# Query parts stored once and repeated on loading, the value ring in the place of projection weights, and the first maximum pass planned into phase one

## The chip, the cores and the metric

The kernel runs on one core of a Trainium2 chip. Its engines are named as in the profile: PE (TensorE, matrix products; PEld is its loading of weights), DVE (VectorE), ACT (ScalarE), POOL (GpSimd) and SP (SyncE), which here issues every DMA. The metric is device time in microseconds of one execution. Beside it the profile gives the granted clock of TensorE, as a share of full speed.

## The reference

The reference is one decoder block over 32 sequences `b` of 128 positions by 512 features, with three layer normalisations, each after a residual sum:

```python
x = _layernorm(x + _L0_attn_ref(x, Wq, Wk, Wv, Wo))
x = _layernorm(x + _L0_xattn_ref(x, ctx_2048, ctx_2048, gamma))
x = _layernorm(x + _L0_ffn_ref(x, w1, b1, ln_g, ln_b, w2, b2))
```

- `_L0_attn_ref` is causal self-attention with 16 heads of 32 features and rotary positions.
- `_L0_xattn_ref(q, k, v, gamma)` works across features: the 128 positions are cut into 8 heads of 16, and in each head `einsum('bhdq,bhdl->bhql')` contracts those 16 positions, so the scores of a head are 512 by 512. Softmax over the last axis, then `einsum('bhql,bhdl->bhdq')`; keys and values are both the context.
- `_L0_ffn_ref` is a feed-forward layer of 512 to 2048 to 512 with weights rounded to -1, 0, 1 and activations rounded to 8 bits; SiLU, exact GELU and a layer normalisation lie between its two products.

## The kernel before

The work is in two phases, each written out as operations with a kind, a planned cost, a priority and their buffers (`pl.op("PE.mx", cost, fn, ins, outs, prio)`). A list scheduler (class `Plan`) orders them: of all kinds' next operations it takes the one with the earliest planned start, in steps of `slack`, and between equals the one of lowest priority; to the priority it adds an offset for the kind from the tables `OFF1` (phase one) and `OFF2` (phase two). It emits the instruction at once, and then fixes the order on every engine. So on the chip each engine runs a fixed list in order, and SP's list of DMAs is one of them. Every DMA issue waits, besides its own data, for the landing of the DMA eight issues earlier on SP.

**Phase one** (0 to about 563 us) takes the sequences in turn: the projections (L346, PE, `banka`), self-attention (L447 to L500), the output projection with weights wo (L346 again), the residual `ya` (L505), statistics and `x1` (L519, POOL). `x1` is stored as it is in `x1_d` (L521), and by `split3` cut into three bfloat16 parts whose sum is x1: a high part (L354, ACT), a difference (L357, POOL), a second part (L359, ACT), and the rest (L361, POOL), all in one tile `sp`. The parts are stored by L364. The context is split likewise into `k_d` and reshaped into `c_d`. The feed-forward weights are quantised on the side.

A product of two split numbers needs six pairs of parts. The kernel makes them one matrix product with a contraction over 96 rows (6 pairs by 16 positions): it stores the query parts in the order 0, 1, 2, 0, 1, 0 and the context parts in the order 0, 0, 0, 1, 1, 2, so that row block `s` of the one meets row block `s` of the other. So each sequence has six stores of 128 KB to `q_d` and six to `k_d`, and half a sequence (four heads) is loaded by one DMA of 96 rows of 4 KB, 384 KB, into a tile `qp` or `kp` (L656; rings of `NQ` = 4 tiles). Rows 96 and 97 are extra: `kp` has ones there, loaded from `ones_d` (L587), and `qp` gets the negated maxima.

**Phase two** (from about 563 us) works in 64 units, sequence `b` by half `g`. A unit has two passes:

- `b1_`, the maximum pass: 16 products of 96 rows (L677, tile `mx`), 16 maximum reductions on DVE (L681, into `mt`), a transpose on PE (L691), and its negation split into `mhi` and `mlo` (L694, L695), which two DMAs of 4 KB put in rows 96 and 97 of `qp` (L700).
- `b2_`: 16 products of 98 rows (L756, `sT`), which give scores less their maximum; 16 exponentials on ACT (L759, `ex`); products with the value tile `cT` (L766, `acc`), whose second half is set to one by a memset (L616) so that the same product gives the sum of the exponentials; a copy (L773) and a store to `F` (L777).

After the two units of a sequence come the division and layer normalisation (L838 to L848, over `F`, `den`, `rd`, `rden`, `num`), the feed-forward layer (up L925, down L1009, with transposing DMAs `q1T` and `q2T`) and the store of the output.

The seam: when the last projection operation has been planned, a function `early()` runs. It closes the pool of the projection weights wqk and wv, opens the pool `qk` in their place, and issues there the ones and the loads of the first four units:

```python
for i in range(NQ):
    nc.sync.dma_start(k[NPR:NROW], ones_d)
    for t, d in ((k, k_d), (q, q_d))[:2 if i < min(CFG['early'], NQ) else 0]:
        nc.sync.dma_start(t[0:NPR], d[i // 2]...)
```

The other tiles of phase two lie in pools (`smb`, `pb`, `cb`, `psb`) that are opened once phase one has been planned, and so in memory that phase one used. Among them are the three value tiles `cT` (the ring `vring`) with their memsets, in the pool `cb`. A tile there waits for the last instructions and DMAs of phase one that used the memory.

Of the kernel before, what the change touches and what calls it, by code (L numbers as in the profile page):

```python
# [11 lines left out]
F32 = mybir.dt.float32  # L12
# [30 lines left out]
Q_PARTS = (0, 1, 2, 0, 1, 0)  # L43
K_PARTS = (0, 0, 0, 1, 1, 2)
# [19 lines left out]

CFG = dict(y0e='Pool', x2be='Pool', q2T=1, q1=2, tb2=3, boost=1.0, bank_mT='mx', bank_q1T='m', bank_z='m', bank_q2T='mx', bank_py='m', early=5, ssv=1, NQ=4, cT=3, f=2, num=1, x1=2, rden=2, x2=2, nb=32, mx=3, sT=3, acc=1, m=1, ex=8, mTe='DVE', acce='ACT', q1e='ACT', q2e='ACT', lne='Pool', ye='Pool', sce='Pool', mxw=1, stw=1, pair=1, z=3, xb=3, slack=0.05, last_lne='DVE', last_ye='DVE', last_sce='DVE', last_y0e='DVE', last_bank_mT='sT', last_bank_q1T='m', last_bank_z='sT', last_bank_q2T='mx', last_bank_py='sT', zm='PPPP', last_zm='FFFP', q1m='p', q2m='ad', last_q1m='d', last_q2m='ad')
OFF2 = {'SP.const': -264.67, 'x.kq': 390.3, 'SP.v': 77.29, 'PE.mx': -381.13, 'DVE.mx': 126.92, 'PE.mT': -632.22, 'DVE.mT': 8.23, 'SP.m': -156.28, 'PE.sT': -531.43, 'ACT.ex': -687.83, 'PE.pv': 37.38, 'ACT.acc': -737.17, 'SP.f': 49.63, 'SP.fd': 1119.71, 'SP.fn': 725.19, 'SP.fx': 343.0, 'DVE.rd': -172.57, 'SP.fr': -316.31, 'SP.fb': 17.98, 'Pool.y': -355.28, 'DVE.y': -82.99, 'Pool.yn': -277.59, 'DVE.c1': -57.25, 'Pool.c1': -358.01, 'Pool.c1m': -627.03, 'Pool.q1a': -78.8, 'Pool.x2b': 72.59, 'SP.q1T': -375.73, 'PE.c1': 39.79, 'DVE.z': -137.9, 'ACT.gelu': -406.78, 'DVE.nmu': -80.22, 'ACT.sq': -333.32, 'Pool.zn': -48.07, 'Pool.zt': 303.63, 'Pool.zb': -221.61, 'ACT.sq2': 252.58, 'DVE.am2': 91.79, 'Pool.c2': -682.87, 'Pool.c2m': -291.19, 'ACT.q2a': -262.61, 'DVE.q2a': -514.12, 'SP.q2T': 382.04, 'PE.c2': 86.97, 'DVE.c3': 17.23, 'Pool.c3': -278.83, 'Pool.c3n': 302.38, 'SP.out': 77.71, 'SP.kq': -42.69, 'DVE.yn': -735.62, 'DVE.c1m': 785.24, 'DVE.q1a': 467.22, 'DVE.zn': 550.15, 'DVE.zb': -508.13, 'DVE.c2m': -306.12, 'DVE.c3n': 99.96}
OFF1 = {'SP.x': 76.47, 'SP.w': -83.56, 'ACT.w': 1251.46, 'DVE.wl': 97.39, 'DVE.w': 1455.82, 'SP.wq': 258.11, 'ACT.wq': -501.07, 'DVE.wq': -718.11, 'PE.wq': 497.75, 'ACT.xh': -83.03, 'Pool.xl': -493.52, 'PE.qkv': 642.06, 'DVE.rope': -749.29, 'Pool.rope': 726.68, 'ACT.v': -277.88, 'SP.cx': 161.38, 'ACT.cs': 561.27, 'Pool.cs': 151.36, 'Pool.cs3': 444.12, 'SP.cs': -169.59, 'SP.ct': -341.75, 'ACT.ct': 5.76, 'SP.cv': 657.35, 'PE.qkT': -233.53, 'DVE.qkT': -713.26, 'PE.sc': 223.31, 'DVE.mask': -673.03, 'ACT.exp': 343.93, 'DVE.rd': 481.16, 'DVE.pr': 893.48, 'PE.prT': -342.18, 'DVE.prT': 602.51, 'ACT.prT': 121.56, 'Pool.pr': 38.32, 'PE.pv': 403.29, 'ACT.oh': 297.53, 'DVE.ol': -241.16, 'PE.wo': 645.28, 'DVE.y': -873.41, 'Pool.y': 255.11, 'Pool.x1': -113.85, 'SP.x1': 730.76, 'ACT.xs': 299.8, 'Pool.xs': -1039.81, 'Pool.xs3': 582.54, 'SP.xs': 975.4}
C1 = dict(pace=15.0, xs=4, pr=5, prT=7, ra=3, qkT=4, sp=3, spr=2, xhe='ACT', lne='Pool', s1e='Pool', s2e='ACT', cxl=-0.5, wq=3.0, nb=32, wst=4, mm=3, tr=3, sc=4, scc=1.1, po=1, pc=4, spe='ACT', cte='ACT', s3e='Pool', qke='DVE', pre=['DVE', 'DVE', 'Pool', 'Pool'], prTe=['DVE', 'ACT', 'ACT', 'ACT'], wl=24.0, slack=0.02)
# [14 lines left out]
class Plan:  # L83
# [34 lines left out]
    def op(self, kind, cost, fn, ins=(), outs=(), prio=0.0, lat=None, rel=0.0, join=False):  # L118
# [5 lines left out]
        o.deps, o.new = [], []  # L124
# [96 lines left out]
def decoder_kernel(ctx: ExitStack, tc: tile.TileContext, x, xT, cx, cxT, wqkT, wvT, woT, gamma,  # L221
# [28 lines left out]
    q_d = [dram.tile([6, XD, XH, D], BF16, tag=f"qd{b}", name=f"qd{b}") for b in range(NB)]  # L250
    c_d = [dram.tile([P, XD, NC * XH], F32, tag=f"cd{b}", name=f"cd{b}") for b in range(NB)]
    k_d = [dram.tile([6, XD, XH, D], BF16, tag=f"kd{b}", name=f"kd{b}") for b in range(NB)]


    with ExitStack() as st1:
# [38 lines left out]
        for name in ("mm", "tr", "sc", "po"):  # L294
            pl.tag(name, C1[name], group="bank")
        pl.tag("part", 2, wts, (P, 16))

        def dma(kind, fn, kb, ins=(), outs=(), prio=0.0, rel=0.0):
            pl.op("SP." + kind, max(0.55, kb / 340), fn, ins, outs, prio, 2.2 + kb / 340, rel)
# [38 lines left out]
        def project(kind, pq, parts, w, sl, wb, prio):  # L338

            steps = [(a, t, c) for a, t in ((0, 0), (1, 0), (0, 1)) for c in range(NC)]  # L340
            m = C1['pc']
            for i in range(0, 12, m):
                def mm(i=i):
                    for k in range(i, i + m):
                        a, t, c = steps[k]
                        nc.tensor.matmul(pq.t, parts[a].t[:, c, :], w[t][:, c, sl], start=k == 0, stop=k == 11)  # L346
                used = [parts[0]] + ([parts[1]] if i + m > 4 else [])
                pl.op("PE." + kind, 0.236 * m, mm, used + [wb], (pq,), prio)

        def split3(kind, v, dst, parts, prio):  # L350
# [12 lines left out]
            for s, k in enumerate(parts):  # L363
                dma(kind, lambda s=s, k=k: nc.sync.dma_start(dst[s].rearrange("t h c -> h t c"), sp.t[:, k, :]), 131,  # L364
                    (sp,), (), prio)

        def context(b):
# [3 lines left out]
            split3("cs", t, k_d[b], K_PARTS, at)  # L371
# [114 lines left out]
        def stage_o(b):  # L486
# [35 lines left out]
            split3("xs", x1, q_d[b], Q_PARTS, at)  # L522
# [46 lines left out]
        for b in range(NB1):  # L569
            stage_q(b)  # L570
            context(b)
            stage_s(b)
            stage_o(b)
        pl.slack = C1['slack']
        NQ = CFG['NQ']
        kring, qring = [], []

        def early():

            st2.close()  # L580
            qk = pool(ctx, "qk", side="right")
            for i in range(NQ):
# [5 lines left out]
                for t, d in ((k, k_d), (q, q_d))[:2 if i < min(CFG['early'], NQ) else 0]:  # L588
                    nc.sync.dma_start(t[0:NPR], d[i // 2][:, :, 4 * (i % 2):4 * (i % 2) + 4, :].rearrange(
                        "s t h c -> (s t) h c"))  # L590
# [3 lines left out]
    sm2 = pool(ctx, "smb")  # L594
# [10 lines left out]
    NB2 = CFG['nb']  # L605
    NQ = CFG['NQ']
# [6 lines left out]

    vring = [cb.tile([P, 2 * XD, NC * XH], F32, tag=f"cT{i}", name=f"cT{i}") for i in range(CFG["cT"])]
    for t in vring:
        nc.gpsimd.memset(t[:, XD:], 1.0)  # L616
    pl.tag("cT", CFG["cT"], ring=vring)
    pl.tag("kp", NQ, ring=kring)
    pl.tag("qp", NQ, ring=qring)
    pl.tag("zq", 64, ring=[None] * 64)  # L620
    for name, shape, dtype in (
            ("mt", (P, 16), F32), ("mhi", (16, P), BF16), ("mlo", (16, P), BF16),
# [21 lines left out]
    Q, K, V, X2 = {}, {}, {}, {}  # L644

    def load(b):
        at = b
        for g in range(2):
            K[b, g], Q[b, g] = k, q = pl.buf("kp"), pl.buf("qp")
            h = slice(4 * g, 4 * g + 4)  # L650

            first = 2 * b + g < min(CFG['early'], NQ)

            def fetch(t, d, h=h, first=first):
                if not first:
                    nc.sync.dma_start(t.t[0:NPR], d[b][:, :, h, :].rearrange("s t h c -> (s t) h c"))  # L656
# [3 lines left out]
            dma("kq", lambda k=k, fetch=fetch: fetch(k, k_d), 393, outs=(k,), prio=at, rel=30.0 * b - 40.0)  # L660
            dma("kq", lambda q=q, fetch=fetch: fetch(q, q_d), 393, outs=(q,), prio=at, rel=30.0 * b - 40.0)
        V[b] = v = pl.buf("cT")
        dma("v", lambda: nc.sync.dma_start(v.t[:, 0:XD], c_d[b]), 262, outs=(v,), prio=at + 0.5, rel=30.0 * b)

    def b1_(b, g):

        at = b + 0.5 * g
        k, q = K[b, g], Q[b, g]
        mt, W = pl.buf("mt"), CFG['mxw']

        def unit(h, qc):
            sc = pl.buf("mx")
            p = at + 0.5 * (4 * h + qc) / 16

            def scores():
                for j in range(W):
                    nc.tensor.matmul(sc.t[:, j, :], q.t[0:NPR, h, (qc + j) * P:(qc + j + 1) * P], k.t[0:NPR, h, :],  # L677
                                     start=True, stop=True)
            pl.op("PE.mx", 0.222 * W, scores, (q, k), (sc,), p)
            i = 4 * h + qc  # L680
            pl.op("DVE.mx", 0.064 + 0.534 * W, lambda: nc.vector.tensor_reduce(mt.t[:, i:i + W], sc.t, AX.X, ALU.max),  # L681
                  (sc,), (mt,), p, join=True)
        for h in range(4):
            for qc in range(0, NC, W):
                unit(h, qc)
        shift(b, g, mt, at + 0.5)

    def shift(b, g, mt, at):

        hi, lo, pt, q = pl.buf("mhi"), pl.buf("mlo"), bank(b, 'mT'), Q[b, g]  # L690
        pl.op("PE.mT", 0.2, lambda: nc.tensor.transpose(flat(pt)[0:16, 0:P], mt.t, ident), (mt,), (pt,), at)  # L691

        def parts():
# [8 lines left out]

    def last(b):
        return b >= NB2 - CFG['tb2']

    def slow(b):

        return 2.0 if b >= NB2 - 2 else 1.0

# [375 lines left out]
```

## Time and profile before

| | |
|---|---|
| three runs | 1674.02, 1676.19, 1684.5 us; median 1676.19 |
| the profiled execution | 1675.28 us, its span 1673.5 us, granted clock 0.973 |
| PE busy | 1551.4 us, 93% of the span |
| ACT, DVE, POOL busy | 1432.7 (86%), 1383.9 (83%), 1251.5 us (75%) |
| DMA | 258.71 MB, 155 GB/s in the mean; 192 stores `qd<-sp` and 192 `kd<-sp` of 128 KB, 64 loads `qp<-qd` and 64 `kp<-kd` of 384 KB |

The page gives one execution. The span runs from the first to the last instruction; the execution's own time is 1.8 us longer. A row of a window table names a stretch of the span, then for each engine the microseconds it was busy in it and how many instructions it ran, the granted clock, the mean busy share of the 16 DMA engines and their rate. A line of waits names who waited, for whom, the sum in us, how often, and the longest. A line of a timeline gives start and length in us, the engine (SPq is SP issuing a DMA), the line in the kernel, the operation, its output and inputs, and how many such instructions in a row. Where one engine's in-order list holds an instruction that waits, all behind it wait too.

### The profile page before, as it was taken

How to read it: one execution, taken by the hardware profiler on the slowest of the kernel's cores; microseconds unless marked ns; L12 is line 12 of the kernel's file. 1: busy time of each engine (PE TensorE's matmuls, PEld its weight loads, DVE VectorE, ACT ScalarE, POOL GpSimd, SP SyncE). 2: the span in 40 equal slices, each digit the busy share in tenths (PEclk: the TensorE clock that was granted, in tenths of full speed). 3: DMA queues.
4: the chain of work that ended last, by engine and by line, in shares of the span. 5: the costliest groups of instructions: out<-in, count | busy, mean ns of one | idle time of the engine just before them, and what ended most of it. 6: DMA issues, size and time to landing. Idle time of an engine off the chain costs nothing.

```text
span 1673.5 us, 30270 instructions
## 1 busy us (share of the span) xinstructions
PE 1551.4 (93%) x9540; PEld 785.0 (47%) x9540; DVE 1383.9 (83%) x3315; ACT 1432.7 (86%) x2950; POOL 1251.5 (75%) x1679
## 2 busy tenths in 40 slices
PE   6999999999999799999999999999999999999844
PEld 4878777777778333333333333333333333333211
DVE  6877776777777678899999989899899999998674
ACT  4889989899976367999989989899999999998963
POOL 3777778777787404679879888878978888986772
PEclk8999999999999799999999999999999999999977
DMA  6476677766664654355455345545544544544221
GB/s 226 163 236 232 226 231 244 255 233 214 209 208 153 185 177 122 93 129 145 113 133 147 105 129 139 131 115 139 142 110 128 153 110 134 149 122 123 69 62 50
DMA packets 235680, 258.71 MB, mean 155 GB/s; under 512 B 110072, under 2 KB 159224, under 8 KB 235136
## 3 DMA queue, kind: packets, MB, share of 16 engines
q1 hardware_dynamic: 235520, 256.78, 52.8%
q8 instruction: 75, 1.23, 0.3%
q14 instruction: 85, 0.70, 0.1%
HBM read 142.41 MB, written 92.81 MB: 141 GB/s over the span
## 4 chain that ended last, share of the span: by engine, by line
PE 41%; DVE 18%; POOL 16%; DMA 9%; ACT 8%; issue 7%; SPq 1%; POOLq 0%; ACTq 0%; DVEq 0%
PE banka L346 12%; DVE mt L681 8%; PE acc L766 7%; PE sT L756 6%; POOL z L972 6%; PE mx L677 5%; PE m L925 2%; DVE am L998 2%; PE banka L477 2%; DMA qd<-sp 2%; POOL z L794 2%; PE banka L447 2%; ACT pr L465 1%; ACT ex L759 1%; PE banka L496 1%
## 5 line engine op out<-in xcount | busy, mean ns | idle before, releaser
L681 DVE TENSOR_REDUCE mt<-mx 128x1 f32<-128x512 f32 x1024 | 643.4, 679 | 54.9 <-PE mx L677 52.9
L759 ACT ACTIVATE ex<-sT 128x512 f32<-128x512 f32 x1024 | 533.9, 615 | 77.9 <-PE sT L756 74.4
L677 PE MATMUL mx<-kp,qp 96*128 96x512 bf16 x1024 | 336.9, 386 | 21.5 <-DVE mt L681 17.7
L756 PE MATMUL sT<-qp,kp 98*128 98x512 bf16 x1024 | 320.7, 385 | 15.9 <-DMA qp<-mlo 13.3
L766 PE MATMUL acc<-ex,cT 128*32 128x512 f32 x2048 | 289.4, 637 | 0.0
L465 ACT ACTIVATE pr<-pr,nm 128x128 f32<-128x128 f32 x512 | 198.9, 394 | 4.1 <-DVE nm L459 4.1
L756 PEld LDWEIGHTS <-kp 98*128 98x128 bf16 x1024 | 90.3, 98 | 223.7 <-issue 125.1
L677 PEld LDWEIGHTS <-qp 96*128 96x128 bf16 x1024 | 96.3, 98 | 195.5 <-issue 95.1
L972 POOL TENSOR_TENSOR z<-z,bb_b 128x512 f32<-128x512 f32 x119 | 154.4, 1301 | 0.3
L972 POOL TENSOR_TENSOR z<-z,g_b 128x512 f32<-128x512 f32 x119 | 153.5, 1297 | 0.5
L459 DVE CUSTOM_DVE_ANT_0 pr<-banka,cmask 128x128 f32<-128x128 f32 x512 | 111.0, 286 | 35.9 <-PE banka L447 35.2
L1009 PE MATMUL m<-w2q,q2T 128*128 128x512 fp8e4 x464 | 116.7, 385 | 16.4 <-DMA q2T<-q 16.4
L766 PEld LDWEIGHTS acc<-ex,cT 128*32 128x32 f32 x2048 | 70.6, 184 | 114.1 <-issue 108.8
L925 PE MATMUL m<-w1q,q1T 128*128 128x512 fp8e4 x464 | 119.1, 378 | 2.7 <-DVE z L928 1.3
L1009 PEld LDWEIGHTS <-q2T 128*128 128x128 f16 x512 | 51.0, 101 | 104.5 <-DMA q2T<-q 34.9
L465 ACT ACTIVATION_READ_ACCUMULATOR pr<-pr,nm 128x1 f32 x512 | 98.0, 191 | 0.0
L794 POOL TENSOR_SCALAR z<-z,nmu,rs 128x512 f32<-128x512 f32 x119 | 94.5, 801 | 1.8
L361 POOL TENSOR_TENSOR sp<-spr,sp 128x512 bf16<-128x512 f32 x64 | 76.7, 1200 | 20.3 <-ACT sp L359 18.2
L928 DVE SCALAR_TENSOR_TENSOR z<-m,dq,b_b 128x512 f32<-128x512 f32 x116 | 85.0, 733 | 1.8 <-PE m L925 1.5
L925 PEld LDWEIGHTS <-q1T 128*128 128x128 f16 x512 | 49.2, 97 | 76.1 <-issue 19.9
L846 POOL TENSOR_TENSOR num<-num,rden 128x512 f32<-128x512 f32 x29 | 37.1, 1278 | 62.3 <-DMA rden<-rd 62.2
L346 PE MATMUL banka<-wqkh,xh 128*128 128x512 f32 x256 | 73.9, 411 | 10.3 <-ACT xh L388 10.3
(152 smaller groups left out, 3247.9 us busy)
## 6 DMA issues: line engine op xcount, KB each, us to landing
kd<-sp SPq DMA_DIRECT2D x192, 128.0 KB
qd<-sp SPq DMA_DIRECT2D x192, 128.0 KB
kp<-kd SPq DMA_DIRECT2D x64, 384.0 KB
qp<-qd SPq DMA_DIRECT2D x64, 384.0 KB
F<-f SPq DMA_DIRECT2D x64, 256.0 KB
xt<-in_xT SPq DMA_DIRECT2D x32, 256.0 KB
xs<-in_x SPq DMA_DIRECT2D x32, 256.0 KB
ct<-in_cxT SPq DMA_DIRECT2D x32, 256.0 KB
```

What stands on the lines that cost most here:

```text
L346: nc.tensor.matmul(pq.t, parts[a].t[:, c, :], w[t][:, c, sl], start=k == 0, stop=k == 11)
L459: nc.vector.tensor_tensor_reduce(pr.t[:, c, :], sc.t[:, c * P:(c + 1) * P], cmask, -1.0, 3e38, ALU.add, ALU.min, nm.t[:, c:c + 1])
L465: nc.scalar.activation(pr.t[:, c, :], pr.t[:, c, :], AF.Exp, scale=-1.0, bias=nm.t[:, c:c + 1], accum_out=den.t[:, c:c + 1])
L677: nc.tensor.matmul(sc.t[:, j, :], q.t[0:NPR, h, (qc + j) * P:(qc + j + 1) * P], k.t[0:NPR, h, :], start=True, stop=True)
L681: pl.op("DVE.mx", 0.064 + 0.534 * W, lambda: nc.vector.tensor_reduce(mt.t[:, i:i + W], sc.t, AX.X, ALU.max), (sc,), (mt,), p, join=True)
L756: nc.tensor.matmul(sc.t[:, i, :], k.t[:, h, lc * P:(lc + 1) * P], q.t[:, h, :], start=True, stop=True)
L759: pl.op("ACT.ex", 0.052 + 0.426 * SW, lambda: nc.scalar.activation(ex.t[:, j:j + SW, :], sc.t, AF.Exp, scale=1.0 / XD ** 0.5), (sc,), (ex, ...
L766: nc.tensor.matmul(acc.t[32 * h:32 * h + 32, :], v.t[:, :, XH * lc + 4 * g + h], exs[h // 2].t[:, h % 2, :], start=lc == 0, stop=lc == NC - 1)
L794: pl.op(e + "." + p, cost + 0.1, lambda: en(e).tensor_scalar(o.t[:, sl], v.t[:, sl], sh.t, sc.t, ALU.add, ALU.mult), ins, outs, prio)
L925: nc.tensor.matmul(flat(pz)[:, i * 512:(i + 1) * 512], q1T.t[:, c, :], w1q[:, c, (n + i) * 512:(n + i + 1) * 512], start=c == 0, stop=c == ...
L972: pl.op(e + kind, 0.148 + 0.0021 * w if e == "Pool" else 0.05 + 0.00105 * w, lambda: en(e).tensor_tensor(t(), t(), other[:, sl], op), src, ...
L1009: nc.tensor.matmul(flat(py)[:, 0:D], q2T.t[:, c, :], w2q[:, c, :], start=c == 0, stop=c == NI - 1)
```

## The change

Three things are changed, and with them the planned order.

1. `q_d` holds each of the three query parts once, so a sequence has three stores to it and not six. A unit's query tile is filled by three DMAs: part 0 three times (48 rows), part 1 twice (32 rows), part 2 once (16 rows). The repetition is made by the DMA's source pattern (`to_broadcast`). The row blocks of `qp` now hold parts 0, 0, 0, 1, 1, 2, and the context parts are stored in the order that fits; there are still six context stores, grouped by part.
2. The value tiles `cT` with their memsets are made in `early()`, in the memory of wqk and wv, ahead of the ones.
3. The loads of the first four units are operations of phase one's plan and no longer issued inside `early()`, and the maximum pass of the first unit (`CARRY` = 1) is planned in phase one too, with phase one's PSUM banks. The pool `smb` with `mt`, `mhi`, `mlo` is opened at the start for that.

The offsets of all kinds in `OFF1` and `OFF2` have new values, the planned costs of the projection, of the stores and of the loads are changed, and the order of instructions on the engines differs throughout. The counts of instructions on PE, DVE, ACT and POOL do not change.

```diff
-Q_PARTS = (0, 1, 2, 0, 1, 0)
-K_PARTS = (0, 0, 0, 1, 1, 2)
+Q_TIMES = (3, 2, 1)
+K_ROWS = (slice(1, 6, 2), slice(0, 5, 4), slice(2, 3))
...
-    q_d = [dram.tile([6, XD, XH, D], BF16, tag=f"qd{b}", name=f"qd{b}") for b in range(NB)]
+    q_d = [dram.tile([3, XD, XH, D], BF16, tag=f"qd{b}", name=f"qd{b}") for b in range(NB)]
...
+    def load_k(t, b, g):
+        nc.sync.dma_start(t[0:NPR], k_d[b][:, :, 4 * g:4 * g + 4, :].rearrange("s t h c -> (s t) h c"))
+
+    def load_q(t, b, g):
+        r = 0
+        for k, n in enumerate(Q_TIMES):
+            nc.sync.dma_start(t[r * XD:(r + n) * XD],
+                              q_d[b][k, :, 4 * g:4 * g + 4, :].unsqueeze(0).to_broadcast([n, XD, 4, D]))
+            r += n
...
-                pl.op("PE." + kind, 0.236 * m, mm, used + [wb], (pq,), prio)
+                pl.op("PE." + kind, 0.244 * m, mm, used + [wb], (pq,), prio)
...
-            for s, k in enumerate(parts):
-                dma(kind, lambda s=s, k=k: nc.sync.dma_start(dst[s].rearrange("t h c -> h t c"), sp.t[:, k, :]), 131,
-                    (sp,), (), prio)
+            for k, rows in enumerate(parts):
+                def put(k=k, rows=rows):
+                    for d in range(*rows.indices(6)):
+                        nc.sync.dma_start(dst[d].rearrange("t h c -> h t c"), sp.t[:, k, :])
+                n = len(range(*rows.indices(6)))
+                pl.op("SP." + kind, 0.55 * n, put, (sp,), (), prio, 2.2 + 0.4 * n)
...
-            split3("cs", t, k_d[b], K_PARTS, at)
+            split3("cs", t, k_d[b], K_ROWS, at)
...
-            split3("xs", x1, q_d[b], Q_PARTS, at)
+            split3("xs", x1, q_d[b], [slice(k, k + 1) for k in range(3)], at)
...
+        for i in range(NQ):
+            b, g = divmod(i, 2)
+            K[b, g], Q[b, g] = pl.buf("kp"), pl.buf("qp")
+            for t, load_, kind in ((K[b, g], load_k, "cs"), (Q[b, g], load_q, "xs")):
+                pl.op("SP.kq", 1.2, lambda t=t, load_=load_, b=b, g=g: load_(t.t, b, g), (), (t,), NB1 + b + 0.5 * g, 3.4,
+                      after=pl.kinds["SP." + kind][3 * b:3 * b + 3] + pl.kinds["PE.qkv"][-1:])
+            if i < CARRY:
+                b1_(b, g, NB1 + b + 0.5 * g)
...
         def early():
...
             qk = pool(ctx, "qk", side="right")
+
+            for i in range(CFG["cT"]):
+                t = qk.tile([P, 2 * XD, NC * XH], F32, tag=f"cT{i}", name=f"cT{i}")
+                nc.gpsimd.memset(t[:, XD:], 1.0)
+                vring.append(t)
             for i in range(NQ):
...
                 nc.sync.dma_start(k[NPR:NROW], ones_d)
-                for t, d in ((k, k_d), (q, q_d))[:2 if i < min(CFG['early'], NQ) else 0]:
-                    nc.sync.dma_start(t[0:NPR], d[i // 2][:, :, 4 * (i % 2):4 * (i % 2) + 4, :].rearrange(
-                        "s t h c -> (s t) h c"))
...
-    vring = [cb.tile([P, 2 * XD, NC * XH], F32, tag=f"cT{i}", name=f"cT{i}") for i in range(CFG["cT"])]
-    for t in vring:
-        nc.gpsimd.memset(t[:, XD:], 1.0)
...
     for b in range(NB2):
         load(b)
         for g in range(2):
-            b1_(b, g)
+            if 2 * b + g >= CARRY:
+                b1_(b, g, b + 0.5 * g)
```

## The prediction

> **What bounds the kernel now.** I read the windows first, one for each stage, with busy time by engine, granted TensorE clock and DMA share:
>
> ```profile
> 100.00:540.00 440.00, 430.20 (x3554) 344.15 (x3553) 319.76 (x1342) 391.13 (x1248) 340.92 (x397) 1.00 0.68 225
> 549.00:564.00 15.00, 12.65 (x88) 9.39 (x87) 8.33 (x17) 10.09 (x34) 11.77 (x16) 1.00 0.87 223
> 564.00:586.00 22.00, 13.48 (x27) 2.31 (x26) 15.61 (x29) 1.24 (x2) 6.05 (x10) 0.54 0.56 190
> 640.00:1500.00 860.00, 833.99 (x4344) 297.59 (x4343) 796.50 (x1349) 800.77 (x1207) 715.79 (x1015) 0.99 0.49 128
> ```
>
> The first number after the stretch is its length, the next PE's busy time. Phase one (first row) and steady phase two (last) are PE's: 98% and 97% busy, 9.8 and 26 us idle. Only the seam between the phases stands still: in 564 to 586 ACT works 1.2 us of 22. So I read the waits of that stretch, then SP's timeline in it:
>
> ```profile
> POOL cT L616 <- DMA qd<-sp: 9.1, 1, 9.1
> PE sT L756 <- DMA qp<-mlo: 7.1, 1, 7.1
> POOL x L519 <- DMA x1d<-x: 2.8, 1, 2.8
> ```
>
> ```profile
> 572.05 5.31 SPq L364 DMA_DIRECT2D qd<-sp  x8
> 582.37 0.33 SPq L663 DMA_DIRECT2D cT<-cd  x1
> 582.75 0.62 SPq L700 DMA_DIRECT2D qp<-mhi  x1
> 583.42 0.57 SPq L700 DMA_DIRECT2D qp<-mlo  x1
> ```
>
> VectorE has unit 0's maxima (mhi, mlo) ready at 574.87, but their two small transfers stand in SP's queue behind eight qd stores and the cT load, which waits for POOL's memset, which waits for the last qd stores to land. They issue 7.9 us late; PE's first sT starts at 585.55, ACT's first exp at 586.22, unit 1's first sT at 598.62. The change aims at this stall.
>
> **Transfers by packets.** Stores that go and loads that come must be priced by how many of the 16 DMA engines they use. In the trace's packet records every transfer ends in 4-byte completion packets. A 256 KB transfer over 128 rows on both sides, such as x, posts 16 and, alone, takes 0.83 us (34 cases); num and rden, equally large but with an outermost size of 8, post 8 and take 1.93 us (6 cases); a qd or kd store (128 partitions into 8x16x512) posts 8 and takes 1.05 us. The four ones loads have two rows. If a transfer posts the largest number up to 16 that divides both outermost sizes (8, 16, or 2 for the ones), and a transpose 32, all issues make 17,528; with gamma's 128 data packets of 4 bytes that is 17,656, and the trace has 17,657. So the count follows the outermost sizes. And narrow transfers share the same engines: while a row of qd stores is in flight (562 to 573 us) mostly 8 or 9 of their packets run at once, never more than 11.
>
> The new query loads read one part with a leading repeat of 3 or 2. By that count they get 3, 2 and (the third) 16 engines: 48 and 32 rows of 4 KB make 16 packets each on the first engines, and the third 1. That is 33 packets per unit where now there are 6. A 4 KB packet takes 159 ns at the 10th percentile, 209 at the median, 318 at the 90th.
>
> The Trainium skill, "DMA: Bandwidth & Descriptors", section "Why a DMA increments its semaphore by 16 and not by 1", states this divisor rule and that SP's transfers take the lowest-numbered engines; its "Rules for kernel authors" say a leading zero-stride broadcast of c copies confines a transfer to at most c engines. The trace agrees for 8 (17,656 counted, 17,657 found); a zero-stride source no run here shows. By the rule the sum is the forecast below; without it, on 16 engines, it would be the first rival's.
>
> **Part by part.**
>
> *Query parts stored once.* 96 stores go: 96 x 0.576 us of issue = 55 us of SP, and per sequence 3 x 16 packets from the first eight engines. PE waits for nothing of that kind: its whole idle time in 100 to 540 is 9.8 us, mostly softmax turns. Gain between 0 and 9.6 us; I take 3, nearer the low end, since PE's named waits there are ACT and VectorE. The new offsets reorder phase one too, and could also take such an amount.
>
> *Three loads for one, steady state.* 60 units x 2 more issues x 0.42 us = 50 us of SP over 1,000 us; SP issues about 20 transfers in the 31.6 us of a sequence and has room. The first engines have less. Mean DMA share 0.49 x 31.6 = 15.5 us; less 12 query packets (2.5), plus 1.9 because num and rden lie on eight engines, gives 14.9. Two units add 66 packets: 10.5 us at 159 ns (80% busy), 13.8 at 209 ns (91%). Every other transfer has a share on those engines and queues behind up to 7 us of query rows. The sensitive one is mlo: in half the units PE's first sT starts only 1.3 to 3 us after its issue, the least possible. In the new order PE's work between maximum transpose and first sT grows (median 8.8 to 10.2 us, counting 0.216 us per product), and through b = 15 both load groups follow the tight unit's mlo and precede the slack one's, which has 7 to 12 us. So the order covers most of it. If all mlo and max waits of PE went (6.2 + 1.7), -8; if half of the 30 sequences lost 1.7 us, +25. I take +3: cover is there, but thin at units 1 to 6, where that lead is 1.6 to 6.5 us.
>
> *Memory and memsets moved.* Memset (1.45 us of POOL) now waits for the last projection matmul and lies under the last wo matmuls; the cT load no longer stands ahead of mhi and mlo. If that cover failed, one prT would be 1.45 us late. But ACT's first exp, PE's first acc and the first F store still wait for the last qd stores, as their tiles overlay phase one's.
>
> *First maximum pass in phase one.* Its first two products stand in PE's order ahead of the last two pr transposes, and need all of unit 0's loads. SP's new order is four ones, then sixteen loads for four units, then x1d29, qd28, x1d30, qd29, qd30, x1d31, mhi, mlo, qd31; and each issue also waits for the landing of the one eight before. On the first engine a unit costs 6 x 0.209 + 33 x 0.159 = 6.5 us, or 8.2 all at 209 ns; four cost 26 to 33. From 552: unit 0 at 558.5 to 560, so wo 31 ends about 4 us later than 562.6; the last loads at 578 to 585. x1d29 lands behind them (+0.8); x1_31 reuses its tile, as in the wait of 2.8 us above, and runs at 580 to 586 (before 568.86). x1d31 waits for it, mhi and mlo stand behind x1d31: first sT 583 to 589. sp's parts (3.8 us, 569.6 to 573.4 before), qd31's last issue (0.6) and landing (about 2): first exp 586.5 to 592.5. Then 13 exps of 0.615, six reduces of 0.65 and the transpose, split and mlo (3.8): unit 1's first sT 602 to 608, because before, ten of its sixteen products were done inside the stall. Against 598.62: +4 to +10, I take +6. If the loads spread over 16 engines, everything lands as now (12.7 us for these 3.1 MB), x1_31 comes at 567, first exp 575, unit 1 at 590: -8.
>
> **Sum**, against the profiled execution (1675.28 us, span 1673.5): -3 + 3 + 6 = +6, 1681; the median of the three runs is 0.9 higher: **1682**.
>
> **Rivals.**
> 1. *The loads use 16 engines, or land early enough* (the stall goes). For it: 96 destination rows as before, and 7.9 us plainly lost to queue order. Against: the completion counts. 1676 - 8 - 3 - 2 = 1663.
> 2. *Slower: the first engines saturate in phase two.* Their work reaches the 31.6 us of a sequence when a 4 KB packet takes (31.6 - 14.9) / 66 = 0.253 us. At 0.29 each sequence costs 2.4 us more, 30 make 73; with half the sequences affected, 1676 + 36 = 1712. For it: the 90th percentile of 318 ns. Against: those are packets of transfers on 16 engines at the full 250 GB/s; three engines alone should see 159.
> 3. *The redrawn order decides.* Offsets of all kinds are new, and 26 us of PE idle in phase two and the start (16.5 us idle in the first 50) could move either way by 10: 1666 or 1692.
> 4. *Hidden anyway:* loads quick, but the first exp still waits for qd31: 1675.
>
> **Chances.** Forecast 0.52, rival 1 0.15, rival 2 0.17, rival 3 0.1, rival 4 0.06. One per cent is 16.8 us, about what a measurement of this kernel can tell from none. Faster than 1659 needs rival 1 or 3 with luck: 0.12. Slower than 1693: rival 2 and the forecast's upper end: 0.28. Within: 0.60. The range takes in rival 1 and reaches rival 2's middle: 1657 to 1712.
>
> **What the new profile would show.** Packets of qp loads two or three at a time; in SP's timeline pauses between the sixteen loads; x1_31 (L604) waiting on x1d until about 580; first exp at 586 to 593, unit 1's first sT after 600; in steady state the DMA share spread thin while PE's waits on mlo stay near 6 us. I am wrong if four units' loads are down by 563, if PE waits on mlo or query loads for tens of us (rival 2), or if phase one alone shortens by more than 10 us.

## The result, and the profile after

The changed kernel takes 1788.04 us (median of four runs, 1784.41 to 1799.91), the kernel before 1675.11 beside it: ratio 1.0681, interval 1.061 to 1.0751. It is 113 us slower. The forecast was 1682, its range ended at 1712.

The windows of the changed kernel, in the stretches that were shown of before (the number after the stretch is its length, the next one PE's busy time; at the end granted clock, DMA share and GB/s):

```profile
100.00:540.00 440.00, 433.20 (x3619) 345.69 (x3617) 324.21 (x1339) 388.01 (x1230) 338.59 (x398) 1.00 0.60 197
549.00:564.00 15.00, 8.95 (x57) 5.39 (x58) 6.47 (x12) 3.73 (x7) 8.53 (x11) 0.77 0.47 132
564.00:586.00 22.00, 6.23 (x21) 2.45 (x21) 8.20 (x16) 3.20 (x6) 5.36 (x8) 0.65 0.41 138
640.00:1500.00 860.00, 775.01 (x3896) 272.33 (x3894) 714.47 (x1211) 716.59 (x1080) 638.80 (x904) 0.95 0.52 116
```

Phase one is a little faster (PE 433 of 440 us, where it was 430). The seam still stands, and has moved earlier: PE worked 12.7 of the 15 us from 549 to 564 before, now 9. And in steady phase two PE has lost 59 of 860 us, with the DMA share higher (0.52, was 0.49) while the bytes moved fall (116 GB/s, was 128): the DMA engines are longer at less work. PE's granted clock fell there as well, from 0.99 to 0.95, and one of its instructions takes 0.199 us in the mean (775.01 us over 3896), before 0.192 (833.99 over 4344). By an estimate from these two rows, 27 of the 860 us went into slower products, beside the waits.

The steps, in us from the start of the span, put the loss in its place. "Widened" is the first experiment below.

```
                           before    changed    widened
last projection ends        549.1      542.3      544.9
first exp                   586.2      584.7      573.2
unit 1's first exp          599.3      604.3      592.4
last exp                   1590.6     1698.8     1580.8
unit 1 to last exp          991.3     1094.5      988.4
```

So about 5 us were lost by unit 1, and 103 after it, 3.3 us in the mean for each of 31 sequences. Waits of the changed kernel for transfers, 640 to 1500, those of over 5 us (who, for whom, sum, times, longest; one more, 61.9 us of POOL before the first `num`, is left out, since it began at 581):

```profile
POOL num L870 <- DMA rden<-rd: 56.2, 12, 16.8
PE mx L301 <- DMA qp<-qd: 24.0, 9, 5.8
PE acc L790 <- DMA cT<-cd: 14.2, 6, 7.4
PEld acc L790 <- DMA cT<-cd: 13.5, 4, 8.4
POOL x2b L936 <- DMA out<-x2b: 12.9, 4, 4.0
DVE den L865 <- DMA den<-F: 12.9, 6, 7.6
PEld L1033 <- DMA q2T<-q: 7.8, 3, 4.0
PEld L301 <- DMA qp<-qd: 6.1, 2, 4.7
PE m L1033 <- DMA q2T<-q: 5.9, 3, 3.1
```

Before, the longest waits for transfers in that stretch, and the only one for query loads, were these:

```profile
POOL num L846 <- DMA rden<-rd: 12.9, 5, 9.2
PEld L756 <- DMA qp<-mhi: 9.1, 7, 2.9
DVE den L841 <- DMA den<-F: 8.9, 8, 2.3
PE sT L756 <- DMA qp<-mlo: 6.2, 6, 2.5
PEld L677 <- DMA qp<-qd: 0.8, 1, 0.8
```

PE waited for query loads once, and for value loads not at all. What is missing after the change is the line PE sT <- mlo: PE no longer waits there for the one transfer that the prediction watched, and waits for others. SP's timeline shows how; it is the worst case of 32:

```profile
858.02 0.38 SPq L281 DMA_DIRECT2D kp<-kd  x1
858.46 2.33 SPq L286 DMA_DIRECT2D qp<-qd  x3
861.80 0.31 SPq L281 DMA_DIRECT2D kp<-kd  x1
862.15 1.83 SPq L286 DMA_DIRECT2D qp<-qd  x3
864.10 11.15 SPq L1027 DMA_TRANSPOSE q2T<-q  x1
875.29 0.58 SPq L746 DMA_DIRECT2D cT<-cd  x1
875.99 0.58 SPq L325 DMA_DIRECT2D qp<-mhi  x1
```

Two units' loads are issued in 6 us, and the transposing DMA behind them holds SP for 11.15 us. From 640 to 1500 the issue of `q2T` takes 5.5 us in the mean, before 3.4 (longest 6.4).

That the loads are narrow is to be read in the completions. The trace has 17,209 packets of 4 bytes, 448 fewer than before. 96 stores less, of 8 completions each, take away 768; 64 units with 3 + 2 + 16 completions in place of 16 add 320; the sum is -448 exactly. Steady 4 KB packets take 162 ns at the median, and for 230 of the 860 us two or three of them are in flight at once (before: 18 us). The records don't name a packet's engine; which transfers are held up is read from their landings below.

### The profile page after: what moved, and what is told of

It reads as the page before. It is cut to its first block, busy times and chain, and to the rows that moved or that the text cites. A ratio compares the mean times of both kernels' runs of the same rounds, so it can differ in the third digit from the quotient of the medians.

```text
span 1782.6 us, 30334 instructions
## 1 busy us (share of the span) xinstructions
PE 1584.7 (89%) x9540; PEld 790.6 (44%) x9540; DVE 1393.1 (78%) x3315; ACT 1434.7 (80%) x2950; POOL 1247.4 (70%) x1679
## 4 chain that ended last, share of the span: by engine, by line
PE 42%; DMA 19%; POOL 16%; DVE 11%; ACT 5%; issue 4%; SPq 3%; POOLq 0%; ACTq 0%; DVEq 0%
PE banka L428 13%; PE acc L790 6%; POOL z L996 6%; PE mx L301 6%; PE sT L780 5%; DMA rden<-rd 5%; DVE mt L305 4%; DMA qp<-qd 3%; PE m L1033 3%; PE banka L562 2%; DMA cT<-cd 2%; POOL z L818 2%; SPq L286 2%; PE banka L581 2%; PE m L949 2%
## 5 line engine op out<-in xcount | busy, mean ns | idle before, releaser
L305 DVE TENSOR_REDUCE mt<-mx 128x1 f32<-128x512 f32 x1008 | 636.4, 679 | 107.5 <-PE mx L301 104.3
L301 PE MATMUL mx<-kp,qp 96*128 96x512 bf16 x1008 | 342.2, 398 | 57.7 <-DVE mt L305 27.9
L780 PE MATMUL sT<-qp,kp 98*128 98x512 bf16 x1024 | 324.9, 389 | 20.7 <-DMA qp<-mlo 11.3
L790 PE MATMUL acc<-ex,cT 128*32 128x512 f32 x2048 | 296.4, 654 | 18.1 <-DMA cT<-cd 18.1
L1033 PE MATMUL m<-w2q,q2T 128*128 128x512 fp8e4 x464 | 127.2, 412 | 23.8 <-DMA q2T<-q 23.8
L870 POOL TENSOR_TENSOR num<-num,rden 128x512 f32<-128x512 f32 x29 | 38.0, 1309 | 123.1 <-DMA qp<-mhi 61.9
L499 POOL TENSOR_TENSOR ra<-ra,rb 128x256 f32<-128x256 f32 x64 | 47.7, 745 | 74.8 <-DVE rb L494 67.8
L1022 DVE TENSOR_REDUCE am<-z 128x1 f32<-128x2048 f32 x32 | 72.9, 2277 | 29.4 <-POOL z L996 29.2
L832 POOL TENSOR_SCALAR rsa<-mv 128x1 f32<-128x1 f32 x64 | 13.4, 209 | 114.3 <-DVE mv L826 101.8
```

The source lines that it names most:

```text
L301: nc.tensor.matmul(flat(sc)[:, j * D:(j + 1) * D], q.t[0:NPR, h, (qc + j) * P:(qc + j + 1) * P], k.t[0:NPR, h, :], start=True, stop=True)
L780: nc.tensor.matmul(sc.t[:, i, :], k.t[:, h, lc * P:(lc + 1) * P], q.t[:, h, :], start=True, stop=True)
L790: nc.tensor.matmul(acc.t[32 * h:32 * h + 32, :], v.t[:, :, XH * lc + 4 * g + h], exs[h // 2].t[:, h % 2, :], start=lc == 0, stop=lc == NC - 1)
L1033: nc.tensor.matmul(flat(py)[:, 0:D], q2T.t[:, c, :], w2q[:, c, :], start=c == 0, stop=c == NI - 1)
```

## The experiments

Two theories. **Narrow**: loads with a leading repeat run on 3 and 2 engines, hold these for 33 packets per unit, and transfers with a share on them that are issued behind these packets land late. **Order**: the redrawn order, the number of issues, or the pass moved into phase one.

### Width, number, order, dose

`e1_wide`, the changed kernel widened: a row of the tile is now 3t+r, not 16r+t.

```diff
-            nc.sync.dma_start(t[r * XD:(r + n) * XD],
-                              q_d[b][k, :, 4 * g:4 * g + 4, :].unsqueeze(0).to_broadcast([n, XD, 4, D]))
+            src = q_d[b][k, :, 4 * g:4 * g + 4, :]
+            src = src.unsqueeze(1).to_broadcast([XD, n, 4, D]) if WIDE[k] else src.unsqueeze(0).to_broadcast([n, XD, 4, D])
+            nc.sync.dma_start(t[r * XD:(r + n) * XD], src)
```

(`WIDE` is 1 for the parts with n = 3 and 2; the context stores get rows to match, by `rearrange("(t r) h c -> r t h c", r=n)`)

> The changed kernel with the repeated rows of the query tile interleaved by position (row 3t+r in place of 16r+t), so that the source's outermost size is 16 and not 3 or 2, and the context rows stored to match. Same transfers, bytes and order on every engine; each of the three query loads should post 16 completions. If the narrow loads are the cause: nearly all of the 113 us goes, 1655 to 1680 us, and the seam is shorter than in the kernel before. If the redrawn order or the pass moved into phase one is the cause: it stays at about 1785. If the number of loads (two more issues in each of 60) is the cause: it stays above 1740.

Measured 1665.33 us, ratio to before 0.9947 (0.9926 to 0.9968). Two swapped dimensions take back 123 us. Its completions are 18,937: 17,657 - 768 + 64 x 32, sixteen for each load. Its row of steady phase two:

```profile
640.00:1500.00 860.00, 837.60 (x4359) 299.55 (x4359) 796.18 (x1351) 800.13 (x1202) 720.51 (x1024) 0.99 0.50 129
```

PE's clock is 0.99 again, and one of its instructions takes 0.192 us, so the slower products of the changed kernel came with the narrow loads.

`e2_before_narrow`, the kernel before with its order, stores and seam, and only the loads replaced by narrow ones:

```diff
-                if not first:
+                if not first and d is q_d:
+                    load_q(nc, t.t, d[b], g)
+                elif not first:
                     nc.sync.dma_start(t.t[0:NPR], d[b][:, :, h, :].rearrange("s t h c -> (s t) h c"))
```

(`load_q` makes three transfers with leading repeats of 3, 2 and 1; the first four units' loads and the rows of the stores are changed to match)

> The kernel before, with its order, its six stores and its seam, but each query load made by three transfers with a leading repeat of 3, 2 and 1 (the context parts stored in the rows that fit). If the narrow loads are the cause: 80 to 130 us slower than before, 1755 to 1805. If the redrawn order is: within 10 us of 1675. The seam alone should lose 5 to 10 us, as the first four units' loads then end about 575.

Measured 1819.82 us, ratio 1.0849 (1.0807 to 1.089): slower still than the changed kernel, a little over the upper end expected. Its seam lost more than the 5 to 10 us expected too: the first exp came at 600.0, 13.8 us later than before. Here the late transfer is mlo:

```profile
PE sT L782 <- DMA qp<-mlo: 57.4, 20, 5.2
```

So the redrawn order did protect mlo (57 us against none). From unit 1 to the last exp this kernel takes 1111.1 us, 17 more than the changed one: with narrow loads the new order is worth that much there, and could not protect all.

`e3_before_wide3`, the same with the repeated dimension inside, so three wide loads:

> As the run before it (three query transfers per unit in the kernel before), but with rows interleaved by position, so that each uses 16 engines. It prices the number of transfers alone. If the engines' width is the cause: within 10 us of 1675, at most 1685. If SP's issues or the eight transfers in flight are: near the narrow version, above 1740.

Measured 1673.62 us, ratio 1.0003 (0.9987 to 1.002). The 128 more issues cost nothing that can be measured. This kernel and the one before it have the same order, stores, bytes and number of transfers and differ in the layout of the rows alone: 1820 and 1674 us.

`e4_half`, the changed kernel with the two-fold part wide and the three-fold part narrow:

> The changed kernel with the two-fold part interleaved (16 engines) and the three-fold part left narrow (3 engines): 19 packets of 4 KB per unit on the first engines in place of 33. If the loss comes only when these engines saturate: most of it goes, under 1700. If the loss is waiting in line behind the narrow rows, in proportion to them: about half is left, 1715 to 1745. If width does not matter: 1785.

Measured 1718.18 us, ratio 1.0252 (1.0222 to 1.0283). Unit 1 to last exp is 1032.5 us: 44 over the widened version, where 33 packets cost 106. The widened version has 6 packets a unit on the first engines; with 13 more, in place of 27 more, four tenths of the loss is left. That fits a price that grows with the rows in line, and not one that begins when engines are full.

### Line or engine

`e9_act_queue`, the changed kernel with phase two's narrow loads issued by ACT:

```diff
-            nc.sync.dma_start(t[r * XD:(r + n) * XD],
+            (nc.sync if 2 * b + g < NQ else nc.scalar).dma_start(t[r * XD:(r + n) * XD],
```

> The changed kernel with its narrow query loads, those of phase two issued by ACT's own queue in place of SP's (ACT waits in order for their tiles and pays the issues). If the others were late because they stood behind the narrow rows in SP's line on the same engines: transfers from SP land as in the kernel before (value loads about 3.6 us after issue in place of 7.9) and the time falls below 1740 in spite of ACT's extra work. If the engines themselves are short of time: landings and time stay as they are, 1780 or more.

Measured 1823.51 us, ratio 1.0863. The time alone tells little, since ACT now waits 45.8 us in order for those loads. The landings tell more. They come from the trace: the time from a transfer's issue to its last completion, medians in us, 640 to 1500, for the transfers that changed most and for mlo.

```
              before   changed   ACT's queue   half   widened
qp<-qd          5.07      8.14          8.66   6.49      4.45
cT<-cd          3.56      7.92          8.48   5.71      4.02
q2T<-q          5.28      8.27          8.56   6.10      5.01
qp<-mlo         1.70      2.55          2.47   2.27      1.73
```

Value loads and transposes, still SP's, land as late as when the narrow rows were ahead of them in SP's own line; another queue does not help. The same bytes in wide rows (last column) delay these transfers little, so it is not the bytes that hold them up; that leaves time on the few engines. Not all transfers are late: `kp`, `num`, `den`, `rden`, `x` and `out` land within 0.3 us of before at the median in the changed kernel (`rden` in the mean 5.6 us, before 4.5). How much of the 103 us comes from late landings themselves, and how much from SP being held in the issue of `q2T`, no run separates.

### What the rest of the change is worth

`e5_six_stores`, the widened version with the extra query copies back, onto the same rows.

> The widened version of the changed kernel with each query part stored three, two and one times (the extra copies onto the same rows, read by nobody), so that phase one has its 96 stores back and nothing else changes. If the fewer stores won phase one's few us: the last projection ends about 549 and not 545, total 1668 to 1672. If the order alone did: within 2 us of 1665.

Measured 1884.38 us, and not for the reason that was tested: in 100 to 540 SP waited 140 us in 52 waits for landing query stores, since two stores to one place are made to wait for each other. It was made again as `e10_six_rows`, each copy with rows of its own:

```diff
-                    for d in range(*rows.indices(6)):
+                    for d in ((0, 3, 5), (1, 4), (2,))[k] if kind == "xs" else range(*rows.indices(6)):
```

> The widened version of the changed kernel with its 96 extra query stores back, each onto rows of its own that nobody reads (an earlier try wrote the copies onto the same rows, so that each store had to await the one before). Order and all else stay. If the fewer stores won phase one's 4 us and shortened the seam: last projection about 549 in place of 545, first exp 580 or later in place of 573, total 1672 to 1680. If they were hidden: within 2 us of 1665.

Measured 1694.73 us, ratio 1.0131, and last projection at 571.1: 26 us later than widened, far more than expected. That the new order has no room in SP's list for 96 more issues is likely, but these runs do not separate it.

`e11_three_stores`, the kernel before in its own order with three stores and three wide loads (a left-out store stays in the plan as an empty operation, so no order changes):

```diff
+                    if kind == "cs" or s < 3:
                         nc.sync.dma_start(
```

> The kernel before in its own order, with three query stores per sequence and three wide query loads per unit: the first part of the change alone, widened. The seam has 12 stores in place of 24 ahead of the maxima's transfers. If the stores set the seam: first exp 578 to 582 in place of 586, total 1664 to 1670. If the last wo and x1 set it: 1672 to 1676.

Measured 1657.98 us, ratio 0.992 (0.9903 to 0.9936), faster than expected. Last projection 539.4 (548.1 with six stores and the same loads, `e3_before_wide3`), first exp 569.9. The stores set both the seam and, against the waits listed, 8.7 us of phase one: loads of x and its transpose land in 2.9 and 3.5 us there, 4.2 and 4.7 with six stores, and ACT's wait for the transposed x, 6.4 us with six stores, is down to 0.5. First the rows with six stores (`e3_before_wide3`), then those with three:

```profile
100.00:540.00 440.00, 428.87 (x3539) 343.28 (x3537) 317.85 (x1335) 387.51 (x1231) 338.18 (x392) 1.00 0.68 223
ACT xh L409 <- DMA xt<-in_xT: 6.4, 6, 1.5
100.00:540.00 440.00, 436.50 (x3654) 352.09 (x3653) 328.01 (x1382) 394.24 (x1263) 345.58 (x402) 1.00 0.61 201
ACT xh L411 <- DMA xt<-in_xT: 0.5, 1, 0.5
```

SP's timeline at its seam:

```profile
555.49 3.94 SPq L386 DMA_DIRECT2D qd<-sp  x6
559.52 0.41 SPq L544 DMA_DIRECT2D x1d<-x  x1
560.06 3.68 SPq L386 DMA_DIRECT2D qd<-sp  x3
566.20 0.32 SPq L691 DMA_DIRECT2D cT<-cd  x1
566.58 0.60 SPq L728 DMA_DIRECT2D qp<-mhi  x1
```

The cT load still stands ahead of the maxima and waits until the last query stores have landed (563.7 to 566.2), since its tile overlays theirs; the next edit removes that.

`e12_vring`, the kernel before with only the value tiles moved:

```diff
+            for i in range(CFG["cT"]):
+                t = qk.tile([P, 2 * XD, NC * XH], F32, tag=f"cT{i}", name=f"cT{i}")
+                nc.gpsimd.memset(t[:, XD:], 1.0)
+                vring.append(t)
...
-    vring = [cb.tile([P, 2 * XD, NC * XH], F32, tag=f"cT{i}", name=f"cT{i}") for i in range(CFG["cT"])]
-    for t in vring:
-        nc.gpsimd.memset(t[:, XD:], 1.0)
```

> The kernel before with the value tiles and memsets made in the memory of the projection weights: the second part alone, in the old order. The cT load ahead of the maxima's transfers no longer waits for the last query stores: first sT about 580 in place of 585.5; but the first exp still awaits the last stores, which land at 582. Total 1671 to 1675. If the memset was the whole wait: first exp 580, total 1668.

Measured 1672.11 us, ratio 1.0001 (0.9985 to 1.0016). mhi went out at 578.17, not 582.75, but the first sT came at 583.3, not at about 580, and the first exp at 584.0. What came last was mlo:

```profile
572.02 5.32 SPq L364 DMA_DIRECT2D qd<-sp  x8
577.45 0.44 SPq L664 DMA_DIRECT2D cT<-cd  x1
578.17 0.62 SPq L701 DMA_DIRECT2D qp<-mhi  x1
578.89 0.56 SPq L701 DMA_DIRECT2D qp<-mlo  x1
PE sT L757 <- DMA qp<-mlo: 4.7, 1, 4.7
```

It was issued 4.5 us earlier than before, and landed only 2.2 us earlier, at 583.21: the eight stores issued ahead of it land 0.7 us apart, the last at 582.22, and cT, mhi and mlo land after them. The small transfers stood behind the stores a second time, in landing. This part was hidden behind the last stores, as the fourth rival had it, but by way of mlo.

`e13_both`, `e11_three_stores` with `e12_vring`:

> The two together in the order of the kernel before: three stores, three wide loads, value tiles moved; neither the pass planned in phase one nor new offsets. If these two parts carry the gain of the widened version: 1660 to 1667, as fast as it or faster. If the redrawn order or the moved pass does: 1668 to 1674.

Measured 1658.09 us, ratio 0.9912 (0.9893 to 0.9931): faster than both kernels, with neither the moved pass nor new offsets. That is a little below the range expected. The median equals that of three stores alone, so the value tiles' move has no gain in the whole that these runs show: unit 1's first exp comes 2.9 us sooner (581.0, not 583.9), and the time from there to the last exp is 2.6 us longer (991.5 and 988.9).

`e6_no_carry`, the widened version with `carry=0`, and `e7_old_offsets`, the widened version with the offset tables of before:

> The widened version with the first unit's maximum pass planned in phase two again; loads, value ring and offsets stay, the planner's order follows. If the moved pass made the seam shorter: first exp after 578 in place of 573, total 1670 to 1676. If the memsets and the fewer stores did: first exp within 2 us, total within 3 us of 1665.

> The widened version with the offset tables of the kernel before (kinds that are new have offset 0). It tells what the redrawn order is worth with wide loads. If order matters little: 1660 to 1675. If the redrawn tables carried the gain: above 1675.

Measured 1697.68 (ratio 1.0137) and 1684.29 us (1.0044). The first does not tell what was asked. Its first exp is at 575.3, only 2 us later than widened, and unit 1's at 588.8, 4 us earlier, so the moved pass shows no gain at the seam. The loss comes later: unit 1 to last exp takes 1008.8 us, 20 more, in a phase two that was planned anew. With old offsets that stretch takes 999.9. The tables drawn for one set of operations did not serve the other here, and the two new plans moved this kernel by 16 and 32 us (by the ratios, against the widened version).

## Why the prediction was wrong

**The seam held in its steps, and in its size by luck.** With narrow loads the prediction put unit 0's loads at 558.5 to 560 (PE's first product came at 554.9, after phase one ended 7 us sooner), x1_31 at 580 to 586 (575.2), first exp at 586.5 to 592.5 (584.7), unit 1's first sT at 602 to 608 (603.9). x1_31 waited behind the four units' loads, by the step that was written down; the chain of waits of the changed kernel has it in one line:

```profile
562.73 12.32 DMA x1d<-x
575.23 0.77 POOL x L604
```

The term "+6", for unit 1's first sT, measured +5.2. But the loads began at 543.6 and not at 552, and unit 0's took 11.2 us from there (landed at 554.8), where 6.5 to 8.2 were worked out. From the last projection to unit 1's first exp the changed kernel takes 62.0 us, the one before 50.2. That is 11.8 more, and the larger gain of phase one made up for it.

Nor was the price of SP's order at the seam quite as it was read. "They issue 7.9 us late" counts the issue alone; `e12_vring` shows that mlo issued 4.5 us sooner lands 2.2 us sooner, while eight stores are still ahead of it.

Without narrowness the prediction put the seam at 575 (first exp) and 590 (unit 1's first sT), and the whole at 1663: the widened version has 573.2, 591.9 and 1665.

**Phase one held in sign, and was sized too low.** "Gain between 0 and 9.6; I take 3". It gained 6.8, and 8.7 where the stores alone were taken out of the old order. The reason given ("PE waits for nothing of that kind") was the wrong reading: no wait of PE named a store, yet with the stores gone inputs landed earlier, and PE was busy 436.5 of the 440 us (428.9 with six stores and the same loads). The trace of before did list a wait that would shorten: ACT's for the transposed x, 5.9 us less, one step ahead of PE. That PE's gain came by that way is argued, not shown; of PE's own listed waits, those of its weight loads for the softmax tiles `pr` and `prT` of ACT became shorter (5.1 to 1.8 and 4.5 to 2.2 us). In the widened version the rest of the change gives 5.5 of it back (544.9 against 539.4).

**The step that failed is the term for steady phase two: "+3 (-8 to +25)".** It measured +103 (991.3 to 1094.5), +106 against the widened version. The prediction's own sign of being wrong came, PE waiting for query loads for tens of us: 24.0 for products and 6.1 for weight loads. Three readings in the term were wrong:

- It priced one victim. "The order covers most of it" was worked out for mlo alone, and for PE's waits on mlo it came true. But cT, q2T and the query loads themselves stand behind the same rows. cT can be issued right after both groups, as in the timeline above, and lands 4.4 us later than before at the median (7.92, was 3.56); with the old order, mlo is the victim. Covering one transfer moved the wait to others.
- Its danger was a threshold. Rival 2 had the right sign and the mechanism's place, but asked for saturation, at 0.253 us a packet. Packets took 0.162 at the median, by the prediction's own sum 14.9 + 66 x 0.162 = 25.6 us of a sequence, and that now lasts about 35: by this estimate the first engines were busy about three quarters of the time. In 186 of the 860 us, moreover, no packet at all is in flight (before: 300). The half dose shows the same, four tenths of the loss with about half of the added rows. Late landings suffice, where the order was planned for loads that land in 5 us.
- So its price came out too small for the same reason: 2.4 us a sequence, 73 us if all were hit, cut to 36 by taking half, 0.17 of chance. The share was nearly right, and the size was not. Against the widened version, which has the same order, 18 of the 31 sequences (from one's first exp to the next one's) became 2.8 to 8.3 us longer, 5.7 in the mean and 102 together; the other 13 changed by -1.2 to 1.8 us.

**The inference on width was right**: 8 completions for 8 rows, so 3 and 2 for leading repeats. The Trainium skill, "DMA: Bandwidth & Descriptors", section "Why a DMA increments its semaphore by 16 and not by 1" and the line on zero-stride broadcasts in "Rules for kernel authors", say it in advance; the completions here now agree (-448 of -448).

**The other rivals**: redrawn order alone is small beside this. With wide loads the whole of the redrawn, moved and re-planned kernel is 0.5% faster than before, and no faster than the old order with the same stores and loads (1665 and 1658, each beside its own runs of before, 1674 and 1672; the intervals of the two ratios touch).

## What to carry to other kernels

Before a transfer gets a repeat, look at the outermost size on both sides: here a repeat outside gave 3 and 2 completions, and inside a dimension of 16 it gave 16, once rows of the tile were renumbered for it. When some engines get long packets in a row, price the landing of every transfer that is issued behind them, and not the busy share or the one transfer that is tight today. And take a bundled change apart with the order held fixed (empty operations in the plan): what paid here was 96 stores less, and the rest of the bundle added nothing that the runs show.

## What was not expected of the hardware

- A transfer issued by another engine's queue was as late as one behind the narrow rows in the same line (value loads 8.48 and 7.92 us, before 3.56): two queues did not keep them apart.
- A transposing DMA behind query loads holds its issuer, and longer when they are narrow: up to 11.15 us for one issue of `q2T` (before: up to 6.4), which takes 1.3 to 2.1 us where nothing is in flight. Why the issue itself waits these runs don't show.
- Fewer stores, of 8 completions each, gave 8.7 us in a phase where PE was 97% busy and none of PE's listed waits named a transfer.
- A transfer of 4 KB issued behind eight stores of 128 KB took 4.3 us to land (mlo in `e12_vring`); with fewer stores ahead, in `e13_both`, it took 1.7.
